# A four-layer graph network in fp32 on one core: order of block products and sums inside the LSTM steps

## The chip, the cores and the metric

The kernel runs on one core of one Trainium2 chip. The metric is the time of one execution on the device in microseconds (us). Five engines work side by side, each through its own list of instructions in order: TensorE (PE in the profile; its weight loads stand as PEld), VectorE (DVE), ScalarE (ACT), GpSimd (POOL) and SyncE (SP), which issues the DMA transfers here. The order of each list is set by the program text: the kernel switches the scheduler off and places every piece by hand.

## The reference, cut to what matters

Four layers, each with layer norm, relu, a graph operation and a residual sum. The change lies in layer 1, two graph convolutions and then, for p = 1 to 4, an LSTM over windows of p tokens whose last state replaces the last token of its window:

```python
h = relu(einsum('ts,bsh->bth', adj, x @ Wg0 + bg0))
h = relu(einsum('ts,bsh->bth', adj, h @ Wg1 + bg1))
for p in range(1, MAX_SKIP + 1):              # MAX_SKIP = 4, H = 256
    nw = Tv // p
    wins = h[:, :nw * p, :].reshape(Bv * nw, p, Hd)
    last = _lstm_last(Wih[p-1], Whh[p-1], bih[p-1], bhh[p-1], wins)
    h = h.at[:, idx, :].set(last.reshape(Bv, nw, Hd))

# one step of the LSTM
g = x_t @ Wih.T + h @ Whh.T + bias
i, f, gg, o = split(g, 4)
c = sigmoid(f) * c + sigmoid(i) * tanh(gg)
h = sigmoid(o) * tanh(c)
```

x has 128 batches of 64 tokens with 256 channels. The kernel cuts them into 16 chunks of 512 columns; two chunks make a superchunk, and the LSTMs of a superchunk run beside the convolutions, residual sums and normalizations of others ("the other stream").

## The kernel before

A gate's product of a 256 x 256 weight matrix with 256 channels is done as seven block products instead of eight, with sums in place of the eighth. A `Unit` is one gate in one step. Gates i and g (numbers 0 and 2) are the A units, f and o (1 and 3) the B units. Each block product has a part with the input x and one with the state h; both go into the same place in PSUM. Products 1, 6, 7 and 4 of a gate accumulate one after another in bank x, product 5 has bank y, products 2 and 3 the halves of bank z. Two banks of each kind are there, so the next gate takes over a bank once its reader is done.

```python
self.of = {1: "x", 6: "x", 7: "x", 4: "x", 5: "y", 2: "z", 3: "z"}

def copy(self, kind):      # ScalarE; kind 1 to block (0, 0), kind 5 to block (1, 1)
    nc.scalar.copy(gate(self.q, kind // 5, halves[kind // 5]), self.psum(kind))

def add(self, dst, a, kind):                                   # VectorE
    nc.vector.tensor_add(gate(self.q, *dst), gate(self.q, *a), self.psum(kind))

def c11(self): self.add((0, halves[0]), (0, halves[0]), 2)     # P1 + P2
def u4(self):  self.add((0, halves[1]), (1, halves[1]), 6)     # P5 + (P1+P6)
def c12(self): self.add((0, halves[1]), (0, halves[1]), 3)     # ... + P3
def c22(self): self.add((1, halves[1]), (1, halves[1]), 7)     # P5 + (P1+P6+P7)
# act(0): ScalarE on c11 and c12; act(1): on c22; act(2): on P1+P6+P7+P4 in PSUM
```

The step, on which all hangs (`each` does one operation for all named units, then the next; `yield` lets the other stream put in a piece):

```python
for s in range(1, p):
    last = s == p - 1
    B = [Unit(q, s) for q in (1, 3)]
    # ... (differences of x for the next step, on GpSimd)
    each(A, pe(5, "h"), do("copy", 5), pe(1), do("copy", 1), pe(3, "h"), pe(6, "x"), pe(6, "h"),
         pe(2, "h"), do("u4"), do("c11"), do("c12"))
    each(B, pe(5), do("copy", 5))
    each(A, do("act", 0), pe(7), do("c22"), do("act", 1))
    each(B[:1], pe(3), pe(2))
    each(A, pe(4), do("act", 2))
    # ... (weights of later steps, when last)
    nc.gpsimd.tensor_mul(gates[:, 0, :, :n], gates[:, 0, :, :n], gates[:, 2, :, :n])
    each(B[1:], pe(3), pe(2))
    each(B, pe(1), do("copy", 1))
    yield
    each(B, pe(6))
    A = [] if last else [Unit(q, s + 1) for q in (0, 2)]
    each(A, pe(5, "x"))

    def cell(c, part):
        nc.vector.tensor_mul(cells[:, c, part], cells[:, c, part], gate(1, c, part))
        nc.vector.tensor_add(cells[:, c, part], cells[:, c, part], gate(0, c, part))
        nc.scalar.activation(gate(2, c, part), cells[:, c, part], AF.Tanh)

    if last:
        each(B[:1], do("u4"), do("c11"), pe(7))
        each(B[1:], do("u4"), pe(7))
        each(B[:1], do("c22"), do("c12"), do("act", 0))
        each(B[1:], do("c22"), do("c11"), do("c12"), do("act", 0))
        cell(0, every)
    else:
        for u in B:
            each([u], do("u4"), do("c11"), do("c12"), do("act", 0))
        cell(0, every)
        each(B, pe(7), do("c22"))
    each(B, do("act", 1))
    each(A[:1], pe(3, "x"), pe(2, "x"))
    new_state(s, 0, every)
    # ... (differences of the state)
    each(A[1:], pe(3, "x"), pe(2, "x"))
    each(B, pe(4))
    B[0].act(2)
    cell(1, halves[1])
    B[1].act(2)
    cell(1, halves[0])
    # ... (the other half's state)
    yield
```

The other stream is placed by the number of the yield. A conversion (`convolutions`) of a chunk goes piece by piece: batch norm and 32 x 32 transposes and a round trip through DRAM; the residual sum; layer norm statistics; its application (twice); a product with the adjacency matrix; its copies; a product with Wg0; a maximum (`bounded`); a product with Wg1; a sum (`biased`); the adjacency again; two relus. `CONV` holds the yields of a superchunk's two chunks, `FIRST` those in the first superchunk, `START` the order of pieces before the first LSTM, `RESIDUAL` those of the residual sum behind the LSTM. With p=1 the yields are 0 to 3, p=2 has 4 to 7, p=3 8 to 13, p=4 14 to 21; even numbers from 6 on are in the middle of a step or in a first product, odd ones at an end.

Of the kernel before, what the change touches and what calls it, by code (L numbers as in the profile page):

```python
# [19 lines left out]
def kernel(  # L20
# [23 lines left out]
    B, T, D = x.shape  # L44
# [544 lines left out]
    with tc.manual_schedule(engines={mybir.EngineType.PE, mybir.EngineType.DVE,  # L589
# [27 lines left out]
        for c in range(2, NCH - 1):  # L617
            a, z = sevens[c], sevens.get(c - 1)
# [146 lines left out]
    with tc.manual_schedule(engines={mybir.EngineType.PE, mybir.EngineType.DVE,  # L765
# [3 lines left out]
        for c in range(2, NCH - 1):  # L769
            a, b, z = sevens[c], sevens.get(c + 1), sevens.get(c - 1)  # L770
# [121 lines left out]
    hTs = {}  # L892
# [146 lines left out]
    def operands_x(p, hv, name, s):  # L1039

        nw, nb, inner, tokens = columns_x(p, hv)
        m = nw * nb // 2
        t = l1.tile([P, 7 * (T // 3) * NB], F32, tag="xd", name=f"xd_{name}_{s}", bufs=2)
        t = [t[:, i * m : (i + 1) * m].rearrange("p (a b) -> p a b", b=inner) for i in range(4)]
        b = {(k, j): tokens(k, s, j) for k in range(KD) for j in range(2)}
        for f in differences(nc.gpsimd, t, b[0, 0], b[0, 1], b[1, 0], b[1, 1]):
            f()
        return {5: t[0], 6: t[1], 7: t[2], 4: t[3], 1: b[0, 0], 2: b[1, 0], 3: b[1, 1]}

    def lstm(p, hv, name, follows, x1, ending):  # L1050
# [3 lines left out]
        n = nb * nw  # L1054
# [32 lines left out]
        halves = [slice(0, m), slice(m, n)]  # L1087
        every = slice(0, n)
# [51 lines left out]
        class Unit:  # L1140
# [31 lines left out]
            def c12(self):  # L1172
                self.add((0, halves[1]), (0, halves[1]), 3)

            def c22(self):
                self.add((1, halves[1]), (1, halves[1]), 7)

# [8 lines left out]
        def each(us, *fs):  # L1186
            for f in fs:
                for u in us:
                    f(u)

        def pe(kind, parts="xh"):
            return lambda u: u.product(kind, parts)

        def do(f, *a):
            return lambda u: getattr(u, f)(*a)

        A = [Unit(q, 1) for q in (0, 2)]
        each(A, pe(5, "x"), pe(3, "x"), pe(2, "x"))
# [3 lines that stand above are left out]
            B = [Unit(q, s) for q in (1, 3)]  # L1202
            if not last:
                ox[s + 1] = operands_x(p, hv, name, s + 1)
            each(A, pe(5, "h"), do("copy", 5), pe(1), do("copy", 1), pe(3, "h"), pe(6, "x"), pe(6, "h"),
                 pe(2, "h"), do("u4"), do("c11"), do("c12"))
            each(B, pe(5), do("copy", 5))
            each(A, do("act", 0), pe(7), do("c22"), do("act", 1))
            each(B[:1], pe(3), pe(2))
            each(A, pe(4), do("act", 2))  # L1210
            if last:
                load_sets(2)
            nc.gpsimd.tensor_mul(gates[:, 0, :, :n], gates[:, 0, :, :n], gates[:, 2, :, :n])  # L1213
            each(B[1:], pe(3), pe(2))
            each(B, pe(1), do("copy", 1))
            yield
            each(B, pe(6))
            A = [] if last else [Unit(q, s + 1) for q in (0, 2)]
            each(A, pe(5, "x"))

            def cell(c, part):
                nc.vector.tensor_mul(cells[:, c, part], cells[:, c, part], gate(1, c, part))
                nc.vector.tensor_add(cells[:, c, part], cells[:, c, part], gate(0, c, part))  # L1223
                nc.scalar.activation(gate(2, c, part), cells[:, c, part], AF.Tanh)  # L1224

            if last:

                each(B[:1], do("u4"), do("c11"), pe(7))
                each(B[1:], do("u4"), pe(7))
                each(B[:1], do("c22"), do("c12"), do("act", 0))  # L1230
                each(B[1:], do("c22"), do("c11"), do("c12"), do("act", 0))
                cell(0, every)
            else:
                for u in B:
                    each([u], do("u4"), do("c11"), do("c12"), do("act", 0))
                cell(0, every)
                each(B, pe(7), do("c22"))
            each(B, do("act", 1))
            each(A[:1], pe(3, "x"), pe(2, "x"))
            new_state(s, 0, every)  # L1240
            if not last:
                dh[0]()
# [6 lines that stand above are left out]
            new_state(s, 1, halves[1])  # L1249
            if not last:  # L1250
                dh[1]()
            new_state(s, 1, halves[0], nc.gpsimd if follows and last else nc.vector)
            if last:
                load_sets(2)
                ending()
            else:
                dh[2]()
            yield
# [145 lines left out]
    def lstms(sc, hT):  # L1404
        hv = hT.rearrange("p k (t b) -> p k t b", t=T)

        names = [f"{sc}_{p}" for p in range(SKIP + 1)]

        def ending(p):

            if p < SKIP:
                operands[p + 1] = operands_x(p + 1, hv, names[p + 1], 1)
            elif sc < NCH // SUP - 1:
                nxt = hTs[sc + 1].rearrange("p k (t b) -> p k t b", t=T)
                operands[1] = block_sums(blocks(sc + 1, nxt), f"{sc + 1}_1")

        yield from single(blocks(sc, hv), names[1], operands.pop(1, None), lambda: ending(1))
        for p in range(2, SKIP + 1):
            yield from lstm(p, hv, names[p], p == SKIP and sc < NCH // SUP - 1, operands.pop(p),
                            lambda: ending(p))  # L1420
# [50 lines left out]

    RESIDUAL = (0, 3, 4), (2, 5, 6)
    CONV = (3, 4, 4, 5, 6, 7, 8, 9, 10, 10), (3, 4, 4, 11, 12, 13, 14, 15, 16, 17, 18, 20)
    BEGUN = (11, 13, 14, 16), (17, 19)
    BEGUN_FIRST = (12, 15, 16, 18), (19, 21)
    FIRST = (1, 3, 3, 4, 4, 5, 6, 7, 8, 9, 10, 11, 12, 12), (3, 6, 7, 8, 10, 13, 14, 15, 16, 17, 18, 19, 20, 20)
    AHEAD = (4, 5, 7, 12, 14, 15), (6, 7)
    LATE = 5, 6, 8, 9  # L1480
    IDLE = {5: 4, 7: 18, 9: 10, 13: 14, 15: 8}
    FINAL = (4, 5, 10, 12, 12, 14), (6, 7, 11, 14, 14, 16)
    START = (0, 1, 0, 0, 0, 1, 0, 1, 1, 0, 0, 1, 1, 0, 1)

    tc.no_sync_barrier()
    with tc.manual_schedule(engines={mybir.EngineType.PE, mybir.EngineType.DVE, mybir.EngineType.Pool,
# [4 lines left out]
        aheads = {c: ahead(c) for c in range(NCH - SUP)}  # L1491
        for n, i in enumerate(START):
            if n == 5:
# [14 lines left out]
    with tc.manual_schedule(engines={mybir.EngineType.PE, mybir.EngineType.DVE, mybir.EngineType.Pool,  # L1508
                                     mybir.EngineType.Activation, mybir.EngineType.SP}):
        last = NCH // SUP - 1  # L1510
        for sc in range(last + 1):
            todo = {}

            def units(places, unit):
                for n in places:
                    todo.setdefault(n, []).append(unit)


            if sc > 1:
                units(LATE[:1], aheads[sc * SUP - 3])  # L1520
            if sc < last:
                for i in range(SUP):
                    units((CONV if sc else FIRST)[i], convs[(sc + 1) * SUP + i])
                new_hT(sc + 1)
            if sc:
                for i in range(SUP):
                    units(RESIDUAL[i], residual((sc - 1) * SUP + i, hTs[sc - 1]))
            else:
                units([0], convs[1])
            if sc > 1:  # L1530
                units(LATE[1:], aheads[sc * SUP - 3])
            if sc:
                for i in range(SUP):
                    units((FINAL if sc == last else AHEAD)[i], aheads[(sc - 1) * SUP + i])
            if sc + 1 < last:
                for i in range(SUP):
                    units((BEGUN if sc else BEGUN_FIRST)[i], convs[(sc + 2) * SUP + i])
            for n, _ in enumerate(lstms(sc, hTs[sc])):
                for u in todo.pop(n, ()):
                    next(u)  # L1540
                if sc == last and n in IDLE:
                    keep_busy(IDLE[n], f"l{n}")
                if sc == last and n == 8:

                    new_hT(sc + 1)
                    for c in range(SUP):
                        load2(c, hTs[sc + 1][:, c, :].rearrange("p (q n) -> p q n", q=Q))
            assert not todo
# [422 lines left out]
    def store(c, t):  # L1971
# [3 lines left out]
        for r in range(2):  # L1975
# [18 lines left out]

    FIRST = """table+0 load2+2 q2+0 copyq2+0 res1+14 res1+15 v2a+0 v2b+0 score2+0 res1+14 res1+15
               exp2+0 q2+1 divide2+0 copyq2+1 load2+3 turn2+0 v2a+1 v2b+1 out2+0 keep+0 res1+14 res1+15
# [15 lines left out]
    with tc.manual_schedule(engines={mybir.EngineType.PE, mybir.EngineType.DVE,  # L2012
                                     mybir.EngineType.Activation, mybir.EngineType.Pool,
                                     mybir.EngineType.SP}):
        run(FIRST, 0)
        close_l1r()
# [61 lines left out]
```

## Time and profile before

| | |
|---|---|
| median of 3 runs | 1889.92 us (1889.86 to 1890.83) |
| span of the profiled execution | 1890.8 us |
| superchunks 1 to 5, from one's p=1 to the next one's | 155.57 us each |
| products of the LSTM steps (L1155) with xd, hd in bank x, 128 columns | 1152 records, 286 and 275 ns |
| weights of the LSTM, DMA | 96 x 960 KB, 6.5 us each |

In the profile L1155 is the product of a unit, L1164 its sum on VectorE, L1161 the copy on ScalarE, L1084 its activation, L1222 and L1223 the cell's multiplication and sum, L1113 the activations of a p's first step, L1126 that step's products. A line of a timeline gives the start, the busy time, engine, line, operation, output and input with shapes, the number of instructions merged, and in brackets the idle time before it and what ended it. TensorE's records overlap: the length of one is not the distance to the next.

### The profile page before, as it was taken

What the parts mean: (1) busy time and instruction counts of PE and PEld (TensorE: products, weight loads), DVE (VectorE), ACT (ScalarE), POOL (GpSimd) and SP (SyncE); (2) the same over time, 40 slices, a digit from 0 to 9 for tenths busy, and PEclk for the clock granted to TensorE, in tenths of its full rate; (3) what the DMA queues carried; (4) which work ended last, traced back from release to release, by engine and by line L of the source; (5) the groups of instructions that cost most, each with busy time, mean ns of one, the idle gap of its engine ahead of it and who ended that gap; (6) DMA issues with size and microseconds to landing.
All of it is one profiled execution on the core that took longest, in us unless ns stands there. A gap on an engine that the chain in (4) does not pass through costs nothing.

```text
span 1890.8 us, 39088 instructions
## 1 busy us (share of the span) xinstructions
PE 1863.0 (99%) x15077; PEld 1479.3 (78%) x15077; DVE 1236.6 (65%) x3150; ACT 1016.6 (54%) x2284; POOL 551.4 (29%) x704
## 2 busy tenths in 40 slices
PE   8999989999999999999999999999999999999998
PEld 6877856886897798699589689878969967777776
DVE  6768845567476666667667666665565567676776
ACT  5766544456456446555655645655565544444453
POOL 5856622122222212212322321222122114332232
PEclk9999999999999999999999999999999999999999
DMA  3224643135333433332433343343144254444433
GB/s 114 73 66 150 234 175 105 49 116 184 106 129 139 151 129 129 110 124 114 151 118 139 141 151 129 129 135 117 52 135 154 71 157 135 143 148 142 139 113 113
DMA packets 111273, 241.45 MB, mean 128 GB/s; under 512 B 11504, under 2 KB 74864, under 8 KB 111088
## 3 DMA queue, kind: packets, MB, share of 16 engines
q1 hardware_dynamic: 110192, 237.09, 37.4%
q8 instruction: 119, 1.95, 0.4%
q0 software_dynamic: 320, 1.05, 0.2%
q10 hardware_dynamic: 576, 0.82, 0.1%
q14 instruction: 66, 0.54, 0.1%
HBM read 170.50 MB, written 68.42 MB: 126 GB/s over the span
## 4 chain that ended last, share of the span: by engine, by line
PE 90%; DVE 5%; ACT 2%; issue 1%; POOL 1%; DMA 1%; SPq 0%; DVEq 0%; ACTq 0%
PE x L1155 23%; PE z L1155 11%; PE g L1126 9%; PE y L1155 6%; PE v L1568 6%; PE x L1329 4%; PE y L1329 3%; PE u L929 3%; PE p_q L1575 3%; PE v L915 3%; PE X L1764 3%; PE X L423 2%; PE X L499 2%; PE Y L1764 1%; PE Y L423 1%
## 5 line engine op out<-in xcount | busy, mean ns | idle before, releaser
L1164 DVE TENSOR_TENSOR gates<-gates,x 128x128 f32<-128x128 f32 (+2 forms) x384 | 118.5, 321 | 326.3 <-PE x L1155 319.1
L1155 PE MATMUL x<-xd,wset 128*128 128x128 f32 (+2 forms) x1152 | 256.8, 311 | 0.7 <-DVE gates L1164 0.2
L1155 PE MATMUL x<-hd,wset 128*128 128x128 f32 (+2 forms) x1152 | 246.7, 303 | 0.0
L1213 POOL TENSOR_TENSOR gates<-gates 128x512 f32<-128x512 f32 (+2 forms) x48 | 75.0, 1562 | 551.8 <-ACT gates L1084 551.8
L1084 ACT ACTIVATE gates<-gates,bias 128x256 f32<-128x256 f32 (+4 forms) x384 | 170.3, 490 | 56.2 <-DVE gates L1164 52.7
L1155 PEld LDWEIGHTS x<-xd,wset 128*128 128x128 f32 x1152 | 180.8, 190 | 19.0 <-DVE gates L1164 6.1
L1155 PEld LDWEIGHTS x<-hd,wset 128*128 128x128 f32 x1152 | 185.1, 191 | 5.0
L1126 PE MATMUL g<-hT,wset 128*128 128x256 f32 (+2 forms) x576 | 183.9, 474 | 1.1 <-DVE hT L1095 1.1
L1126 PEld LDWEIGHTS g<-hT,wset 128*128 128x128 f32 x576 | 108.6, 190 | 69.8 <-issue 38.5
L1161 ACT COPY gates<-y 128x128 f32<-128x128 f32 (+2 forms) x192 | 54.3, 294 | 202.3 <-PE y L1155 201.8
L1155 PE MATMUL z<-hs,wset 128*128 128x128 f32 (+2 forms) x768 | 154.0, 303 | 0.0
L1155 PE MATMUL z<-hT,wset 128*128 128x128 f32 (+2 forms) x768 | 148.4, 306 | 0.0
L1155 PEld LDWEIGHTS z<-hs,wset 128*128 128x128 f32 x768 | 119.8, 191 | 3.3
L1155 PEld LDWEIGHTS z<-hT,wset 128*128 128x128 f32 x768 | 117.9, 192 | 4.4 <-ACT gates L1113 0.5
L1161 ACT COPY gates<-x 128x128 f32<-128x128 f32 (+2 forms) x192 | 56.6, 296 | 93.5 <-PE x L1155 92.8
L1164 DVE TENSOR_TENSOR gates<-gates,z 128x128 f32<-128x128 f32 (+2 forms) x384 | 104.5, 316 | 0.1
L1084 ACT ACTIVATE gates<-x,bias 128x128 f32<-128x128 f32 (+2 forms) x192 | 74.8, 390 | 49.3 <-PE x L1155 46.5
L1113 ACT ACTIVATE gates<-g,bias 128x512 f32<-128x512 f32 (+2 forms) x144 | 74.6, 560 | 30.7 <-PE g L1126 30.2
L1155 PE MATMUL x<-hT,wset 128*128 128x128 f32 (+2 forms) x384 | 85.7, 305 | 0.4 <-ACT gates L1084 0.2
L1155 PE MATMUL x<-hs,wset 128*128 128x128 f32 (+2 forms) x384 | 84.9, 303 | 0.0
L1224 ACT ACTIVATE gates<-cell 128x256 f32<-128x256 f32 (+2 forms) x144 | 55.3, 384 | 51.9 <-DVE cell L1223 50.3
L1155 PE MATMUL y<-xd,wset 128*128 128x128 f32 (+2 forms) x384 | 77.4, 304 | 3.9 <-ACT gates L1113 3.3
(326 smaller groups left out, 4144.6 us busy)
## 6 DMA issues: line engine op xcount, KB each, us to landing
wset<-wfar SPq DMA_DIRECT2D x96, 960.0 KB, 6.5
hT<-far_h SPq DMA_DIRECT2D x124, 128.0 KB, 3.1
far_h<-hm SPq DMA_DIRECT2D x16, 512.0 KB, 2.8
far_n<-xs SPq DMA_DIRECT2D x16, 512.0 KB, 3.5
xs<-far_n SPq DMA_DIRECT2D x64, 128.0 KB, 3.7
far_x<-xs SPq DMA_DIRECT2D x16, 512.0 KB, 3.0
x<-far_x SPq DMA_DIRECT2D x64, 128.0 KB, 3.2
xt<-in_x_dram SPq DMA_DIRECT2D x15, 512.0 KB, 4.1
```

Of the source, the lines that this page charges most:

```text
L423: nc.tensor.matmul(self.banks[tag][:, i * CH // 2 : (i + 1) * CH // 2], w, self.at[kind], start=first and not i, stop=True, skip_group_che ...
L915: nc.tensor.matmul(banks[m], wg0_sb[:, k, m * P : (m + 1) * P], agg[:, k, :], start=(k == 0), stop=(k == KD - 1))
L1084: nc.scalar.activation(gate(q, c, part), src, AF.Tanh if q == 2 else AF.Sigmoid, bias=bs[:, q * KD + c : q * KD + c + 1])
L1113: nc.scalar.activation(columns_of(gate(q, c)), natural(banks[q, c][:, :n].rearrange("p (w b) -> p w b", b=nb)), AF.Tanh if q == 2 else AF. ...
L1126: nc.tensor.matmul(banks[q, c][:, :n].rearrange("p (w b) -> p w b", b=nb), wsets[p, q][:, 2 * k + c, :], hv[:, k, : (nw - 1) * p + 1 : p, ...
L1155: nc.tensor.matmul(folded(self.psum(kind)), wsets[p, self.q][:, BLOCKS[kind][i], :], (ox[self.s] if part == "x" else oh)[kind], start=firs ...
L1161: nc.scalar.copy(gate(self.q, kind // 5, halves[kind // 5]), self.psum(kind))
L1164: nc.vector.tensor_add(gate(self.q, *dst), gate(self.q, *a), self.psum(kind))
L1213: nc.gpsimd.tensor_mul(gates[:, 0, :, :n], gates[:, 0, :, :n], gates[:, 2, :, :n])
L1329: nc.tensor.matmul(folded(ps(g, kind)), wih1[:, g, KINDS1[kind], :], right[kind], start=kind in (2, 5, 1), stop=True, skip_group_check=True)
L1568: nc.tensor.matmul(ps[:, i, :], hT[:, k, j, :], w[:, k, first : first + D], start=(k == 0), stop=(k == KD - 1))
L1764: nc.tensor.matmul(st[c, tag][:, i * CH // 2 : (i + 1) * CH // 2].rearrange("p (a n) -> p a n", n=P), w, st[c, "o7"][kind], start=first an ...
```

## The change

It sets the products and sums of a step in another order; no product is added or removed. For the A units product 2 goes ahead of product 6. For the B units the sums are taken apart: P5 + P3 is formed as soon as P3 is there (`v5`), P1 + P2 (`c11`) as well, and behind product 6 there is one sum alone (`u5`). Product 1 of both goes ahead of products 3 and 2 of the second B unit, so that they stand between products 1 and 6. In the last step product 2 of the second B unit comes behind product 6. The special order of the last step is dropped: sums, activation, product 7, cell and c22 now stand as in the others.

A new yield ("a", counted as a half) behind the A units' products 7 takes VectorE pieces of the other stream that stood at the middle of the step, where they would now be in front of `u5`. In the first superchunk the pieces of chunk 2 begin at the end of `START` instead of at yield 1, and are spread.

```diff
+            def v5(self):
+                self.add((0, halves[1]), (1, halves[1]), 3)
+
+            def u5(self):
+                self.add((0, halves[1]), (0, halves[1]), 6)
@@
-            each(A, pe(5, "h"), do("copy", 5), pe(1), do("copy", 1), pe(3, "h"), pe(6, "x"), pe(6, "h"),
-                 pe(2, "h"), do("u4"), do("c11"), do("c12"))
+            each(A, pe(5, "h"), do("copy", 5), pe(1), do("copy", 1), pe(3, "h"), pe(2, "h"), pe(6), do("u4"),
+                 do("c11"), do("c12"))
             each(B, pe(5), do("copy", 5))
             each(A, do("act", 0), pe(7), do("c22"), do("act", 1))
-            each(B[:1], pe(3), pe(2))
+            yield "a"
+            each(B[:1], pe(3), do("v5"))
             each(A, pe(4), do("act", 2))
@@
-            each(B[1:], pe(3), pe(2))
+            each(B[:1], pe(2))
             each(B, pe(1), do("copy", 1))
+            each(B[:1], do("c11"))
+            each(B[1:], pe(3), do("v5"))
+            if not last:
+                each(B[1:], pe(2), do("c11"))
             yield
             each(B, pe(6))
+            if last:
+                each(B[1:], pe(2))
@@
+            each(B, do("u5"))
             if last:
-                each(B[:1], do("u4"), do("c11"), pe(7))
-                each(B[1:], do("u4"), pe(7))
-                each(B[:1], do("c22"), do("c12"), do("act", 0))
-                each(B[1:], do("c22"), do("c11"), do("c12"), do("act", 0))
-                cell(0, every)
-            else:
-                for u in B:
-                    each([u], do("u4"), do("c11"), do("c12"), do("act", 0))
-                cell(0, every)
-                each(B, pe(7), do("c22"))
+                each(B[1:], do("c11"))
+            each(B, do("act", 0), pe(7))
+            cell(0, every)
+            each(B, do("c22"))
             each(B, do("act", 1))
@@
-    RESIDUAL = (0, 3, 4), (2, 5, 6)
-    CONV = (3, 4, 4, 5, 6, 7, 8, 9, 10, 10), (3, 4, 4, 11, 12, 13, 14, 15, 16, 17, 18, 20)
+    RESIDUAL = (0, 3, 4), (2, 5, 5.5)
+    CONV = (3, 4, 4, 5, 5.5, 7, 8, 9, 10, 10), (3, 4, 4, 11, 11.5, 13, 14, 15, 15.5, 17, 18, 20)
-    FIRST = (1, 3, 3, 4, 4, 5, 6, 7, 8, 9, 10, 11, 12, 12), (3, 6, 7, 8, 10, 13, 14, 15, 16, 17, 18, 19, 20, 20)
+    FIRST = (1, 2, 3, 4, 5, 5.5, 7, 8, 9, 9.5, 11, 12, 12), (3, 5.5, 7, 8, 10, 13, 14, 15, 15.5, 17, 17.5, 19, 20, 20)
-    START = (0, 1, 0, 0, 0, 1, 0, 1, 1, 0, 0, 1, 1, 0, 1)
+    START = (0, 1, 0, 0, 0, 1, 0, 1, 1, 0, 0, 1, 1, 0, 1, 2)
@@
-            for n, _ in enumerate(lstms(sc, hTs[sc])):
+            n = -1
+            for mark in lstms(sc, hTs[sc]):
+                n = n + 0.5 if mark else int(n) + 1
```

## The prediction

> **What bounds the kernel now.** I read the page first: shares of engines, then the chain that ended last.
>
> ```profile
> PE 1863.0 (99%) x15077; PEld 1479.3 (78%) x15077; DVE 1236.6 (65%) x3150; ACT 1016.6 (54%) x2284; POOL 551.4 (29%) x704
> ...
> PE 90%; DVE 5%; ACT 2%; issue 1%; POOL 1%; DMA 1%; SPq 0%; DVEq 0%; ACTq 0%
> ```
>
> TensorE is busy for 99% of the span and carries 90% of the chain. The change removes no product and no sum, so it can only win the time in which TensorE waits. How much is that? The list of waits names few microseconds, so I went to a table of stretches: two of the eight superchunks, and a place in the first one.
>
> ```profile
> 304.00:307.00 3.00, 0.50 (x2) 0.03 (x1) 0.18 (x2) 2.79 (x6) 0.00 (x0) 1.00 0.43 175
> 307.00:311.60 4.60, 4.60 (x16) 2.84 (x16) 2.85 (x5) 3.88 (x7) 0.00 (x0) 0.64 0.76 179
> ...
> 605.68:761.24 155.56, 155.47 (x1091) 126.27 (x1091) 102.03 (x281) 86.75 (x212) 36.36 (x44) 1.00 0.37 131
> 916.81:1072.38 155.57, 155.48 (x1091) 126.28 (x1091) 102.04 (x281) 86.83 (x212) 36.36 (x44) 1.00 0.38 131
> ```
>
> Columns: stretch, length, then PE, PEld, DVE, ACT, POOL with counts, then the granted clock. A superchunk takes 155.56 us, always the same, and PE is busy for 155.47 of it. That is not yet "no waits": a record lasts 0.28 us or longer, while records start 0.11 us apart, so a short wait hides under the record before it. It has to be read from starts. TensorE in the last step of p=4:
>
> ```profile
> 1055.79 0.39 PE L1155 MATMUL x<-hs,wset 128*128 128x128 f32 x2
> 1056.09 0.49 PE L1155 MATMUL x<-xd,wset 128*128 128x128 f32 x2
> ...
> 1056.86 0.39 PE L1155 MATMUL x<-hd,wset 128*128 128x128 f32 x2
> 1057.25 0.49 PE L1155 MATMUL x<-xd,wset 128*128 128x128 f32 x2
> ...
> 1058.02 0.39 PE L1155 MATMUL x<-hd,wset 128*128 128x128 f32 x2
> 1058.34 0.49 PE L1155 MATMUL x<-xd,wset 128*128 128x128 f32 x2
> 1058.67 0.39 PE L1155 MATMUL x<-hd,wset 128*128 128x128 f32 x2
> ```
>
> A product of a block with x or h is two records (passes). Undisturbed pairs start 0.22 us apart. From 1055.79 to 1056.09 it is 0.30 (a wait of 0.07), from 1056.86 to 1057.25 0.39 (0.17), from 1058.02 to 1058.34 0.32 (0.10); and each pair behind a wait takes 0.33, that is 0.10 for starting again. These are P1 to P6 (waits for ScalarE's copy of P1), P6 to P7 (for u4), P7 to P4 (for c22).
>
> I added start-to-start times over the undisturbed 0.112 (128 columns), 0.143 (168), 0.216 (256), over the superchunk at 916.8: 3.66 us lost, of which 0.79 around the convolutions' small products, 0.66 in p=3's steps, 2.07 in p=4's, none in p=2's step; the rest is dust.
>
> VectorE in step 2 of p=4:
>
> ```profile
> 1043.63 0.29 DVE L1164 TENSOR_TENSOR gates<-gates,x 128x128 f32<-128x128 f32 x1 [3.97 <-PE x L1155]
> 1043.84 0.48 DVE L1164 TENSOR_TENSOR gates<-gates,z 128x128 f32<-128x128 f32 x2
> 1044.23 0.28 DVE L1164 TENSOR_TENSOR gates<-gates,x 128x128 f32<-128x128 f32 x1
> 1044.43 0.48 DVE L1164 TENSOR_TENSOR gates<-gates,z 128x128 f32<-128x128 f32 x2
> 1044.89 0.43 DVE L1222 TENSOR_TENSOR cell<-cell,gates 128x256 f32<-128x256 f32 x1
> 1045.42 0.42 DVE L1223 TENSOR_TENSOR cell<-cell,gates 128x256 f32<-128x256 f32 x1
> 1045.76 0.48 DVE L1164 TENSOR_TENSOR gates<-gates,x 128x128 f32<-128x128 f32 x2
> ```
>
> It idles 3.97 us, then has six sums at once (u4, c11, c12 of both B gates), 0.20 us apart, then the cell's two operations, then c22, for which P4 waits. That crowd is what the change thins.
>
> In the first superchunk, the chain:
>
> ```profile
> 304.13 0.06 DVE nmr_b L194
> ...
> 304.72 1.57 ACT cv L196 x3
> 306.29 0.58 ACT gates L1113
> ...
> 307.00 1.18 PE y L1155 x4
> ```
>
> Chunk 2's normalization is late, holds ScalarE, and p=2's first activations release their PSUM banks late: TensorE waits 2.67 us.
>
> **What the Trainium skill says.** "Perfetto Trace Analysis", Identifying the Most-Contended Engine: matmul busy time is no good measure of distance from the limit. The trace agrees: 155.47 busy of 155.56, with 3.66 lost. "TensorE: Matmul & The Clock Gate", What's actually happening: the array falls to half clock after idling for some 3.4 us and needs as long again. Here a wait of 2.67 was enough: the granted clock behind it is 0.64, and eight 256-column passes take 3.46 us in place of 8 x 0.216 = 1.73. "VectorE: DVE Perf Modes", The DRAIN you can't avoid: the next operation starts only when the pipe is empty. The trace shows it less strictly: 128-column sums of 0.28 start 0.20 apart; a dependent pair (mul, add) of 0.43 starts 0.53 apart.
>
> **The change, part by part.** T is the start of the last pass of the first B gate's P6 (gate f, the other is o). Each product is 4 passes.
>
> 1. In steps that are not the last, P3 and P2 of gate o now stand between P1 and P6: 8 passes of 0.112 = 0.89 us more for a copy that was 0.07 late (in the last step P3 alone, 0.45). That wait goes.
>
> 2. VectorE has u5, u5 in place of six sums; P5+P3 and P2 are added before P6. act 0 of f starts after one sum, not three: 2 x 0.20 = 0.40 us sooner, and with it cell and c22. In p=4: P4 is 25 passes after T, 2.79; c22 was done at T+2.79, so 0.06 late; now T+2.41. That wait goes (step 1 of p=3 too, 0.20), and the next step's first waits shrink: at 1047.13 of 0.15 goes, at 1048.32 of 0.30 becomes about 0.2. In p=4's step 2 the wait for u4 behind a conversion (0.32) becomes about 0.1.
> Removed in p=4: three P1-P6 waits (3 x 0.174 = 0.52), two P7-P4 (0.31), 0.22, 0.15 and 0.10; in p=3 two P1-P6 (0.17) and 0.20. Sum 1.67.
>
> 3. The last step of each p (one for p=2, 3, 4) changes against it. Before, c22 stood in front of cell. Now the order is u5, u5, c11 of o (waits for P2, moved behind P6), cell mul, cell add, c22; P4 is only 17 passes after T.
> p=4: P2 of o is complete at 8 x 0.112 + 0.275 = 1.17, c11 starts at 1.21, mul 1.41, add 1.94, c22 2.28 to 2.56, seen by TensorE at 2.62. P4 could start at 1.90: a wait of 0.72 + 0.10. Before: P6-P7 0.27 and P7-P4 0.20, now gone.
> p=3 (pass 0.143, sums 0.32 long and 0.24 apart, mul 0.61 ahead of add): c22 done at 3.09, P4 could start at 2.42: 0.73 + 0.10. Before 0.29.
> p=2 (pass 0.216, sums 0.42 and 0.33 apart, mul to add 0.79): c22 done at 4.30, P4 could at 3.67: 0.68 + 0.10. Before 0.
> New: 0.82 + 0.83 + 0.78 = 2.43; old, gone: 0.47 + 0.29 = 0.76. Cost 1.67.
>
> 4. Convolution sums moved from middle to the "a" place: VectorE reaches them behind A's c22 as before, since B's new sums come later. Zero by itself; without it part 2 would be lost.
>
> 5. A's P2 before P6: u4 has 12 passes before P7 of g in place of 16, 1.3 us for some 0.65. Zero.
>
> So a steady superchunk: -1.67 + 1.67 = 0.0, give or take 0.5.
>
> 6. First superchunk. Chunk 2's conversion (2 x 0.5 and 1.3 us on VectorE, at 286.54) moves to 274.1, where VectorE idles 5.5 us. Its data then lands some 10 us sooner, sums at place 1, statistics at 2; the normalization no longer holds ScalarE. Gone: 2.67 + 0.19 for restarting, the slow passes 3.46 - 1.73 = 1.73, some 0.3 of the wait at 291.38 (0.46). Sum 4.9.
>
> Total: 1889.9 - 4.9 - 8 x 0.0, and 0.5 for the last superchunk, which has bare step starts (one wait of 0.43): 1884.5.
>
> **Rivals.**
> *The last steps hurt more.* If c22 drags the cell chain and the next p's products wait too, 8 x 3 x 0.3 = 7 us come back: 1891 or above. For: VectorE works in order and c11 of o really stands ahead of the cell. Against: behind p=2 and p=3 stand convolution products of 3.4 us.
> *The last steps hurt less, step starts gain more.* If ScalarE and VectorE chains shorten as a whole, the waits of part 3 may be 0.3 each: 24 x 0.5 = 12 us better, 1872 to 1876. For: the six sums were the only crowd. Against: mul and add must come ahead of c22, and they alone take about 0.9 us.
> *First superchunk's wait only moves.* p=3's start there already waits 0.70 behind statistics; if p=2's products now wait for POOL's differences behind the normalization's power (1.18), only 2 to 3 us are won: 1887. Against: by my count those end near 301.5, needed at 304.4.
>
> **Range and chances.** Each of 24 last steps is uncertain by 0.2 in the same direction (5 us), the first superchunk by 1.5: 1878.5 to 1890.5. All that TensorE waits for in the LSTM stage is about 36 us, 1.9%, so 2% faster is out of reach; 2% slower needs 1.6 us in every last step on top.
>
> **What would show it.** A steady superchunk of 155.1 to 156.0; P6 following P1 at the undisturbed pitch; in last steps a wait of 0.7 before P4 of f; the granted clock at 307 being 1.00. A superchunk under 154.5 means that part 3 is wrong; over 156.5, that it spreads; a wait of over 1 us still at p=2's start, that part 6 is wrong.

## The result, and the profile after

| | before | after |
|---|---|---|
| median of 4 runs each, one chip | 1889.89 us (1889.72 to 1890.83) | 1920.97 us (1920.69 to 1921.01) |
| ratio | | 1.0163, 95% interval 1.0145 to 1.0181 |
| one steady superchunk (at 916.8 us before, at 932.8 us after) | 155.57 us | 160.16 us |
| of it lost between starts of products | 3.66 us | 8.25 us |

The change makes the kernel 1.6% slower. The prediction was 1884.5, with 1878.5 to 1890.5 as its range: the result lies 30 us above its end.

The page of the changed kernel, shares of engines and the chain that ended last:

```profile
PE 1861.0 (97%) x15077; PEld 1475.8 (77%) x15077; DVE 1252.2 (65%) x3150; ACT 1022.2 (53%) x2284; POOL 547.6 (29%) x704
...
PE 85%; DVE 9%; ACT 2%; issue 2%; POOL 1%; DMA 0%; DVEq 0%; SPq 0%; ACTq 0%
```

TensorE does the same 15077 instructions in 1861.0 us (1863.0 before), but its share of the chain falls from 90% to 85%, and VectorE's rises from 5% to 9%. The span is 28 us longer (1918.9 for 1890.8: the LSTM stage is 32.2 us longer, and the later layers are 3.9 us shorter, see the last section), and what was added are waits of TensorE for VectorE. The stretches (columns as in the prediction: PE, PEld, DVE, ACT, POOL, clock) say where:

```profile
303.00:306.00 3.00, 3.00 (x13) 2.27 (x12) 2.52 (x5) 2.07 (x4) 0.00 (x0) 1.00 0.23 71
...
932.77:1092.94 160.17, 155.89 (x1092) 126.02 (x1091) 103.84 (x281) 87.59 (x212) 35.98 (x44) 1.00 0.37 127
```

The second row is a superchunk; the other steady ones are as long, 4.6 us longer than before. The first row is the place in the first superchunk where the kernel before waited 2.67 us and then ran at a clock of 0.64: here TensorE is busy throughout, at full clock. So the part that was counted on works, and something repeats in every superchunk that was not counted at all. The list of waits names it: TensorE's waits for VectorE's sums, with their total in us, their number and the longest. (The list counts only the time in which no record of TensorE runs, so a short wait is missing from it.)

```profile
PE x L1155 <- DVE gates L1164: 19.3, 28, 1.6
...
PE z L1155 <- DVE gates L1164: 17.5, 39, 0.7
```

In the kernel before the first of these rows was 0.2 us, once, and the second was not there. A product in bank x behind a sum is product 4, which waits for c22, or product 7; those of product 4 in the last steps were expected. A product in bank z behind a sum is new. This is gate o in step 1 of p=4 in the kernel before, where the last two passes of product 3 and the first two of product 2 follow each other at 0.22:

```profile
1026.73 0.39 PE L1155 MATMUL z<-hs,wset 128*128 128x128 f32 x2
1026.95 0.39 PE L1155 MATMUL z<-hT,wset 128*128 128x128 f32 x2
```

The same place in the changed kernel, TensorE and VectorE:

```profile
1047.10 0.39 PE L1155 MATMUL z<-hT,wset 128*128 128x128 f32 x2
...
1047.32 0.39 PE L1155 MATMUL z<-hs,wset 128*128 128x128 f32 x2
1047.74 0.29 DVE L1164 TENSOR_TENSOR gates<-gates,z 128x128 f32<-128x128 f32 x1 [0.31 <-PE z L1155]
...
1048.09 0.49 PE L1155 MATMUL z<-hT,wset 128*128 128x128 f32 x2 [0.38 <-DVE gates L1164]
```

The passes at 1047.10 and 1047.32 are product 3. The sum at 1047.74 is v5, P5 + P3. Product 2, at 1048.09, should follow product 3 at 1047.54, and starts 0.54 later, when v5 is done; another 0.10 goes by its restart (its second pair starts at 1048.41, 0.32 behind, in place of 0.22). Product 2 needs nothing of v5. But products 2 and 3 are the two halves of one bank z, and v5 reads one half: the kernel holds the write of product 2 into the other half until that read has ended.

From starts of products, over the superchunk at 932.8, six such waits are new: p=2 0.82 + 0.10; p=3 0.58 + 0.10 and 0.31 + 0.10; p=4 0.60, 0.54 and 0.54, each + 0.10. Together 4.0 us, of the 4.6 that a superchunk grew. For gate o it is the bare way there and back (product 3 ends, v5 runs, product 2 starts: 0.54 at 128 columns). For gate f eight passes of the A units stand between, and still it waits in three of the six steps, because there v5 of f stands behind what was put to place a (in this cut the other stream's sum, L935); these three are 2.0 of the 4.0 us:

```profile
1044.12 1.28 DVE L935 TENSOR_TENSOR cv<-u,c 128x512 f32<-128x512 f32 x2
...
1045.32 0.28 DVE L1164 TENSOR_TENSOR gates<-gates,z 128x128 f32<-128x128 f32 x1
...
1045.65 0.49 PE L1155 MATMUL z<-hT,wset 128*128 128x128 f32 x2 [0.43 <-DVE gates L1164]
```

The last step of p=4, the same place as in the prediction:

```profile
1077.97 0.39 PE L1155 MATMUL x<-hd,wset 128*128 128x128 f32 x2
1078.90 0.49 PE L1155 MATMUL x<-xd,wset 128*128 128x128 f32 x2 [0.55 <-DVE gates L1164]
```

and VectorE in it, behind the two u5 (L1235 and L1236 are the cell's multiplication and sum in this kernel):

```profile
1077.50 0.29 DVE L1164 TENSOR_TENSOR gates<-gates,z 128x128 f32<-128x128 f32 x1
1077.70 0.42 DVE L1235 TENSOR_TENSOR cell<-cell,gates 128x256 f32<-128x256 f32 x1
1078.22 0.43 DVE L1236 TENSOR_TENSOR cell<-cell,gates 128x256 f32<-128x256 f32 x1
1078.57 0.48 DVE L1164 TENSOR_TENSOR gates<-gates,x 128x128 f32<-128x128 f32 x2
```

c11, mul, add, c22, and product 4 waits from 1078.19 to 1078.90: 0.71 + 0.10, as worked out (0.72 + 0.10).

### The profile page after: what moved, and what is told of

Same layout as the page of the kernel before. It is cut to its first block, busy times and chain, and to the rows that moved or that the text cites. A ratio compares the mean times of both kernels' runs of the same rounds, so it can differ in the third digit from the quotient of the medians.

```text
span 1918.9 us, 39091 instructions
## 1 busy us (share of the span) xinstructions
PE 1861.0 (97%) x15077; PEld 1475.8 (77%) x15077; DVE 1252.2 (65%) x3150; ACT 1022.2 (53%) x2284; POOL 547.6 (29%) x704
## 4 chain that ended last, share of the span: by engine, by line
PE 85%; DVE 9%; ACT 2%; issue 2%; POOL 1%; DMA 0%; DVEq 0%; SPq 0%; ACTq 0%
PE x L1155 19%; PE z L1155 11%; PE g L1126 9%; PE v L1577 5%; PE y L1155 5%; PE x L1336 4%; PE y L1336 3%; PE u L929 3%; PE p_q L1584 3%; PE v L915 3%; PE X L1773 3%; PE X L423 2%; PE X L499 2%; DVE gates L1164 2%; PE Y L1773 1%
## 5 line engine op out<-in xcount | busy, mean ns | idle before, releaser
L1155 PE MATMUL x<-hd,wset 128*128 128x128 f32 (+2 forms) x1152 | 254.6, 303 | 0.0
L1155 PEld LDWEIGHTS x<-xd,wset 128*128 128x128 f32 x1152 | 186.6, 191 | 34.5 <-DVE gates L1164 30.0
L1164 DVE TENSOR_TENSOR gates<-gates,z 128x128 f32<-128x128 f32 (+2 forms) x384 | 110.9, 319 | 149.2 <-ACT gates L1161 92.9
L1155 PE MATMUL z<-hs,wset 128*128 128x128 f32 (+2 forms) x768 | 146.5, 303 | 0.2 <-DVE hs L1093 0.2
L1155 PE MATMUL y<-hd,wset 128*128 128x128 f32 (+2 forms) x384 | 79.3, 309 | 0.0
```

The lines of the kernel that those rows point to most:

```text
L1155: nc.tensor.matmul(folded(self.psum(kind)), wsets[p, self.q][:, BLOCKS[kind][i], :], (ox[self.s] if part == "x" else oh)[kind], start=firs ...
```

## The experiments

The theory after this reading: v5 between products 3 and 2 costs 4.0 us per superchunk, the last steps some 2.2, and the rest of the change is a gain. Times are given with their ratio to the kernel before on the same chip, where it took 1891.4 to 1891.9; "superchunk" is the distance between two p=1 starts in the trace.

### r1_p2_with_p3: product 2 directly behind product 3

```diff
-            each(B[:1], pe(3), do("v5"))
+            each(B[:1], pe(3), pe(2), do("v5"))
@@
-            each(B[:1], pe(2))
             each(B, pe(1), do("copy", 1))
@@
-            each(B[1:], pe(3), do("v5"))
-            if not last:
-                each(B[1:], pe(2), do("c11"))
+            if last:
+                each(B[1:], pe(3), do("v5"))
+            else:
+                each(B[1:], pe(3), pe(2), do("v5"), do("c11"))
```

> The changed kernel with product 2 of the B units directly behind product 3 again, both ahead of the sums that read bank z (in the last step product 2 of gate o stays behind product 6). Theory (bank): product 2 waits because the sum v5 still reads the other half of the same PSUM bank; seven waits per superchunk, 0.926 + 0.689 + 0.413 + 0.698 + 0.646 + 0.644 = 4.02 us in six places (0.413 is p=3's second step), vanish: superchunk 160.16 to about 156.1, total 1921 - 8 x 4.0 = 1889. Rival (buffer): bank z is late because its earlier user, an A gate, still holds it; then the wait moves from product 2 to product 3 and the time stays at 1915 to 1922. Rival (crowded VectorE): only the waits of gate f behind the pieces at the place a go, 2.0 of the 4.0: about 1905.

Measured: 1904.04 us (1903.56 to 1904.79), ratio 1.0066 (1.0051 to 1.0081), superchunk 157.67. The time is the one that was named for the rival of a crowded VectorE (1905), but its mechanism is not what the trace shows: that rival leaves the waits of gate o, and the waits before product 2 are gone for both gates. Of 4.0 us only 2.5 came back because new waits appeared, which I had not foreseen. Step 1 of p=4, TensorE:

```profile
1033.20 0.39 PE L1155 MATMUL x<-hd,wset 128*128 128x128 f32 x2
1033.60 0.49 PE L1155 MATMUL x<-hT,wset 128*128 128x128 f32 x2
```

Product 1 of gate f (1033.60) now follows product 4 of the A units at once and takes over their bank x, which ScalarE's act 2 still reads: 0.17 + 0.10, three times in p=4, less in p=3. With a wait before product 4 that grows from 0.27 to 0.40 in step 1 of p=4, this is the missing 1.5 us. In the changed kernel product 2 of f, moved behind the A units' product 4, stood just there as a filler. So that move had a use. It suggests that the order of TensorE is good and only the sum's place is wrong, which r5 tests.

### r3_last_c22_first: c22 ahead of the cell in the last step

```diff
-            each(B, do("act", 0), pe(7))
-            cell(0, every)
-            each(B, do("c22"))
+            if last:
+                each(B, pe(7), do("c22"), do("act", 0))
+                cell(0, every)
+            else:
+                each(B, do("act", 0), pe(7))
+                cell(0, every)
+                each(B, do("c22"))
```

> The changed kernel with c22 ahead of the cell in the last step of each p, as it was before; product 2 stays apart from product 3. Theory: the waits before product 4 (0.785 in p=2, 0.897 in p=3, 0.812 in p=4, 2.49 us per superchunk) shrink to about 0.3 in all: 1921 - 8 x 2.2 = 1903. Rival (the cell's chain is what counts, and a later cell delays the next p): no gain, 1918 to 1923.

Measured: 1904.47 us (1904.07 to 1905.1), ratio 1.0069 (1.0052 to 1.0086), superchunk 157.98: 2.19 us less than in the changed kernel. The last step's part has the size that was predicted for it.

### r4_both_mended: r1 and r3 together

> Both repairs: product 2 directly behind product 3, c22 ahead of the cell in the last step. If both theories hold the gains add up: 1921 - 32 - 18 = 1871, a superchunk near 153.9, faster than the kernel before by 1.0%. If the two waits stand in for each other (TensorE waits for the same late VectorE in either place), about 1889.

Measured: 1887.24 us (1885.88 to 1887.67), ratio 0.9977 (0.9968 to 0.9986), superchunk 155.48. 2.50 and 2.19 add up (160.16 - 155.48 = 4.68 against 4.69): neither wait stands in for the other. The superchunk misses the expected 153.9 by the new waits of r1.

### r2_first_superchunk: only chunk 2's pieces, in the kernel before

```diff
-    FIRST = (1, 3, 3, 4, 4, 5, 6, 7, 8, 9, 10, 11, 12, 12), ...
+    FIRST = (1, 2, 3, 4, 5, 6, 7, 8, 9, 10, 11, 12, 12), ...
-    START = (0, 1, 0, 0, 0, 1, 0, 1, 1, 0, 0, 1, 1, 0, 1)
+    START = (0, 1, 0, 0, 0, 1, 0, 1, 1, 0, 0, 1, 1, 0, 1, 2)
```

> The kernel before with the new start alone: chunk 2's conversion begins at the end of the start, its next pieces at yields 1, 2, 3, 4; nothing else of the change. Theory: 1889.9 - 4.9 = 1885.0 (the wait of 2.67 us at p=2's start, its restart and the slow clock behind it go, superchunks stay at 155.57). Rival (the wait only moves to GpSimd's differences or to p=3's start): 1887 or above.

Measured: 1887.02 us (1885.78 to 1887.83), ratio 0.9976 (0.9967 to 0.9985), which is -4.7 us. (The 1887 of the rival is met only because the kernel before takes 1891.7 us on this chip and not 1889.9.) The same point of superchunk 1's p=1 comes at 445.75 (before at 450.12), and a steady superchunk takes 155.56. The wait of 2.67 at p=2's start, the slow clock behind it and the wait at 291.38 are gone; p=3's start still waits 0.70, as before.

### r5_sums_behind_p2: only two sums moved, TensorE's order as in the changed kernel

```diff
-            each(B[:1], pe(3), do("v5"))
+            each(B[:1], pe(3))
@@
-            each(B[:1], pe(2))
+            each(B[:1], pe(2), do("v5"))
@@
-            each(B[1:], pe(3), do("v5"))
-            if not last:
-                each(B[1:], pe(2), do("c11"))
+            if last:
+                each(B[1:], pe(3), do("v5"))
+            else:
+                each(B[1:], pe(3), pe(2), do("v5"), do("c11"))
```

> TensorE's order is that of the changed kernel, unchanged; only VectorE's v5 (and c11 behind it) of the B units is placed behind product 2 of its gate. Theory (bank: product 2 is held until v5 has read the other half of its bank): all six waits before product 2 go and, unlike with product 2 moved forward, product 1 has product 2 of f ahead of it as in the changed kernel, so nothing new comes: a superchunk of 156.1 us, total 1921 - 32 = 1889. Rival (TensorE's order itself is at fault): 160, 1921.

Measured: 1890.87 us (1890.55 to 1892.26), ratio 1.0001 (0.9992 to 1.0009), superchunk 156.26. The waits of bank z for sums have gone from the list; those of bank x are still there, 34 of them with 21.0 us.

TensorE's list of instructions is that of the changed kernel. Only sums on VectorE stand later, and 30 us are back. That settles where the time went.

### r10_p2_in_another_bank: is it the bank, or the sum's place?

r5 takes the sum away from product 2; it doesn't show that the bank is what joins them. In this run the order of every engine stays that of the changed kernel, v5 between products 3 and 2, and only the place of product 2 of the B gates changes, from bank z to the free half of bank y:

```diff
-                self.banks, self.of = {}, {1: "x", 6: "x", 7: "x", 4: "x", 5: "y", 2: "z", 3: "z"}
+                self.banks, self.of = {}, {1: "x", 6: "x", 7: "x", 4: "x", 5: "y", 2: "yz"[q % 2 == 0], 3: "z"}
@@
-    return self.banks[...][:, m:n] if kind == 3 else ...
+    return self.banks[...][:, m:n] if kind == 3 or (kind == 2 and self.of[2] == "y") else ...
```

> The changed kernel with one edit: product 2 of the B gates goes into the unused half of bank y (in which product 5 stands, long since copied) instead of the half of bank z beside product 3. The order on every engine stays that of the changed kernel; v5 still stands ahead of product 2. Theory (product 2 is held because v5 reads the same bank): the six waits before product 2 go, 4.0 us per superchunk, as when v5 was moved behind it: superchunk 156.2, total about 1890. Rival, that the order itself (v5 early in VectorE's list) costs the time wherever product 2 goes: superchunk stays at 160.1, total 1921.

Measured: 1893.40 us (1892.29 to 1894.66), ratio 1.0011 (1.0004 to 1.0018), superchunk 156.13. Step 1 of p=4, gate o, as above:

```profile
1028.84 0.39 PE L1155 MATMUL z<-hs,wset 128*128 128x128 f32 x2
...
1029.06 0.39 PE L1155 MATMUL y<-hT,wset 128*128 128x128 f32 x2
...
1029.26 0.29 DVE L1164 TENSOR_TENSOR gates<-gates,z 128x128 f32<-128x128 f32 x1 [0.31 <-PE z L1155]
1029.29 0.39 PE L1155 MATMUL y<-hs,wset 128*128 128x128 f32 x2
```

Product 2 (1029.06, now in y) follows product 3 at 0.22, and v5 (1029.26) reads bank z beside it. So the two are joined by the shared bank z, and not by the order. (Each bank is one tile of the program here; the runs don't tell whether the program sets the wait for the bank or for the tile.) The Trainium skill has the rule, in "PSUM — Partial Sum Buffer", PSUM bank collisions raise a hardware error: two engines must not touch one bank on the same partitions at once, disjoint columns included, so "Semaphore-guard PSUM by bank × quadrant". The kernel's waits follow it, and here this one costs 4.0 us per superchunk. What the chip would do without the wait was not tried. (The total is 2.5 us above r5's although the superchunk is shorter: in the traces that lies behind the LSTMs, see the last section.)

### r6_and_c22_first: r5 and r3 together

> As the run before, and c22 ahead of the cell in the last step. Theory: the gains add, as the two waits lie in different parts of a step: 156.1 - 2.2 = 153.9 us per superchunk, total 1871 to 1873, which beats the kernel before by 1%. If they stand in for each other: 1887 or above.

Measured: 1874.75 us (1874.35 to 1875.15), ratio 0.9911 (0.9896 to 0.9926), superchunk 154.09. The two mends add up again (3.90 + 2.17), and the result is 0.9% faster than the kernel before (part of that lies outside of the LSTMs, see the last section). Lost between starts are 2.17 us per superchunk, of which 0.50 before product 4 of p=4's step 1 and 0.32 before product 7 of the A units in its step 2.

### r8_without_place_a: place a undone

r6 (the "second run" of the text below) with the residual sum and the conversion's pieces back at 6, 12 and 16 in place of 5.5, 11.5 and 15.5; the first superchunk keeps its place a.

> As the second run of this call (sums behind product 2, c22 first), but the VectorE pieces of the other stream are put back from the place a to the middle of the step. Theory of the prediction's part 4 (the place a costs nothing and keeps u5 in time): 1.4 to 2.4 us of pieces stand ahead of u5 in three steps, P7 waits 0.4 to 0.8 in each: a superchunk longer by 1.5 to 2, total 1883 to 1888. Rival (the place a is itself the cause of the loss): faster than the second run, below 1871.

Measured: 1890.49 us (1889.86 to 1891.27), ratio 0.9994 (0.9986 to 1.0003), superchunk 156.76: 2.67 more than r6. New waits stand before product 7 in p=2 (0.89), p=3 (0.38) and step 1 of p=4 (0.86), behind VectorE's pieces ahead of u5, and the wait before product 4 there grows from 0.40 to 0.63. So place a is needed for the new order, more than I had put it at.

### r7_and_pieces_moved, r11_application_to_place_a, r9_two_pieces_to_place_a: the last two waits

In r6 ScalarE's application at yield 16 (1.2 us) stands ahead of act 0, and VectorE's conversion at 17 (2.4 us) ahead of u4. The three runs, each r6 with one table changed, move them:

```diff
r6    BEGUN = (11, 13, 14, 16), (17, 19)
r7    BEGUN = (11, 13, 14, 17), (17.5, 19)
r11   BEGUN = (11, 13, 14, 17.5), (17, 19)
r9    BEGUN = (11, 13, 14, 17.5), (17.5, 19.5)
```

> As the run before, and two pieces of the other stream moved in p=4: the normalization's application of the even chunk from yield 16 to 17, the conversion of the odd chunk from 17 to 17.5. Theory: in p=4's first step ScalarE's two applications (1.2 us) stand ahead of act 0, and P4 waits 0.27 to 0.40 + 0.10; in the second step VectorE's conversion (2.3 us) holds u4, and P7 waits 0.22 + 0.10. Both go: 0.7 us per superchunk, 153.2, total some 1867. Rival (these waits come from GpSimd or the state's chain): same as the run before.

Measured: 1886.99 us (1885.03 to 1888.03), ratio 0.9975 (0.9965 to 0.9985), superchunks of 155.9 to 158.6. Both waits went, and two worse ones came. ScalarE at the start of p=4's step 2:

```profile
1035.63 1.09 ACT L196 ACTIVATE cv<-xs,nmr_b,rstd_b 128x256 f32<-128x256 f32 x2 [1.49 <-DVE nmr_b L194]
...
1036.93 0.44 ACT L1161 COPY gates<-x 128x128 f32<-128x128 f32 x2
```

At a step's end the application waits for VectorE, and the copies of product 1, which free bank x for product 6, stand behind it: 1.23 us. And VectorE in step 3:

```profile
1051.69 1.29 DVE L284 TENSOR_TENSOR xs<-xs,cv 128x512 f32<-128x512 f32 x2 [1.90 <-DMA xs<-in_x_dram]
```

The conversion left later, so its data came back later, and the residual sum at 19 held u4 by waiting for it: 1.39 us here, and 1.27 to 2.31 us in the five superchunks that have it.

> r6_and_c22_first with only the application of chunk 0 moved, from the middle of p=4's step 1 to place a of its step 2. Theory: only the wait of 0.40 + 0.10 before product 4 of step 1 goes: superchunk 153.6, total 1871 to 1872; the difference to r9 is the conversion's part (0.32 per superchunk). Rival as for r9: the application holds act 2 of the A units, 1875 or more.

Measured: 1875.98 us (1875.6 to 1876.87), ratio 0.9922 (0.9907 to 0.9937), superchunk 154.34. The wait of 0.40 is gone, but product 1 of gate f waits 0.77 in step 2: the application stands ahead of act 2 of the A units, which frees bank x. That was the rival. (In r1 it was product 1, too, that waited in this way, and not product 4 as the next text says.)

> r6_and_c22_first with three pieces of the coming conversions moved to place a: the application of chunk 0 from the middle of p=4's step 1 to place a of its step 2, the conversion of chunk 1 from the end of step 1 to the same place a, its residual sum from the end of step 2 to place a of step 3. In r7_and_pieces_moved the application at a step's end held ScalarE ahead of the next step's copies of product 1 (1.23 us), and the residual sum reached VectorE before its data did (1.39 us). At a place a neither should be in front of anything. Theory: the waits of 0.40 + 0.10 (product 4 of step 1) and 0.22 + 0.10 (u4 of step 2) of r6 go and none comes: superchunk 153.3, total 1869 to 1870. Rival, that the application now holds act 2 of the A units and through it bank x, as product 4 waited in r1_p2_with_p3: superchunk 154 or more, 1875 or more.

Measured: 1873.47 us (1873.29 to 1873.63), ratio 0.9908 (0.9893 to 0.9923), superchunk 153.83. With the conversion out of the way nmr comes sooner and the application holds act 2 for 0.46 only; of the 0.82 hoped for 0.26 is left. It is the fastest of all, though by the intervals not to be told from r6.

### r12_first_superchunk_place_a: the same in the first superchunk

In r9 the first superchunk takes 157.6 us, counted between the same product of its own p=1 and the next one's, and a steady one 153.8. The first one's conversion at 12 and statistics at 16 are still at the middle of a step, ahead of u5:

```diff
-    BEGUN_FIRST = (12, 15, 16, 18), (19, 21)
+    BEGUN_FIRST = (11.5, 15, 15.5, 18), (19, 21)
```

> r9_two_pieces_to_place_a with two pieces of the first superchunk moved from the middle of a step to its place a: the conversion of chunk 4 (p=3's last step) and its statistics (p=4's step 1). In the changed kernel and in r6 and r9 these two stayed at the middle, where they stand in front of u5: product 7 waits 1.34 + 0.10 and 1.71 + 0.10 us there, in the first superchunk alone. Theory: that is why the first superchunk takes 157.6 us in r9, 3.8 more than a steady one, where the kernel before with the first superchunk's pieces moved (r2) had only 0.9 more. The first wait goes; of the second some 0.6 may stay, because another piece of 1.3 us is at the same place. First superchunk 155.0 to 155.5, total 1871. Rival, that the pieces are too much for VectorE wherever they stand: 157 or more, total 1873 as r9.

Measured: 1877.11 us (1876.65 to 1877.7), ratio 0.9923 (0.9907 to 0.994). The wait of 1.34 went and that of 1.71 became 0.82, as expected. But the first superchunk is longer, 161.0 us. TensorE in p=4's first products, and SyncE's queue before it:

```profile
383.73 2.81 PE L1126 MATMUL g<-hT,wset 128*128 128x256 f32 x8 [3.76 <-DMA wset<-wfar]
```

```profile
371.27 0.32 SPq L247 DMA_DIRECT2D far_y<-ym  x1
374.01 1.74 SPq L254 DMA_DIRECT2D cv<-far_y  x4
...
376.33 2.22 SPq L887 DMA_DIRECT2D wset<-wfar  x4
```

In r9 the first two of these weight loads (L887) are asked for at 369.92, ahead of the conversion's write (375.39). In r12 the conversion's write and its read back, which waits for the write, stand in front of them on SyncE's queue: the weights are asked for 6.4 us later, and TensorE waits 3.9 us for them; after that eight passes start 0.43 apart in place of 0.22. The expectation looked at VectorE alone.

## Why the prediction was wrong

**The step that failed is in part 2: "P5+P3 and P2 are added before P6".** It counted these sums on VectorE, where there was time for them, and let TensorE run on through products 3 and 2. In its place the runs showed that TensorE stands still there: v5 reads bank z between the two, and product 2, which writes the other half of it, waits for v5, six times and 4.0 us per superchunk. r5 (the sums moved, -3.9 us per superchunk) and r10 (the bank changed, -4.0) both give back what was lost. From the first LSTM product to the last the trace takes 1242.1 us before, 1274.3 after, and 1244.4 in r5: 29.9 of the 32.2 us come back in r5. The rivals missed it too: they speak of sums that come too late for their own products, none of a product that waits for a sum that it has nothing to do with. One half of it was there to be read, as the description of the kernel before says that products 2 and 3 have the halves of one bank z, and that the next gate takes over a bank once its reader is done. The step that was missing is that a reader holds the other half of its bank as well.

**Part 1: right.** No product 6 waits for the copy of product 1 any more in p=3 and p=4.

**Part 2, the rest: partly right.** Waits before product 4 in step 2 of p=4 and step 1 of p=3 are gone, and of step 3's first waits 0.31 (0.25 predicted). Two stayed. In step 1 of p=4, P7 to P4 is 0.27 + 0.10, where 0.06 + 0.10 was to go: ScalarE's application at yield 16 stands ahead of act 0, so act 0 doesn't come 0.40 sooner there. The u4 wait of step 2 (0.32) is unchanged; it is the conversion alone that sets it. So about 0.5 of the 1.67 did not come.

**Part 3: right in mechanism and size.** Predicted waits before product 4 of the last steps 0.82, 0.83 and 0.78 for p=4, 3, 2; measured 0.81, 0.90 and 0.78, together 2.49 for 2.43. r3 takes 2.19 of it away. It was accepted in the prediction as balanced by part 2, and r6 shows that it need not be paid.

**Part 4: half right.** "Without it part 2 would be lost" is true (r8: 2.67 us). "Zero by itself", because VectorE's new sums come later, is not: the pieces at place a stand ahead of v5 of gate f, and product 2 of f waits for that in three steps, 2.0 of the 4.0 us. They cost this only together with the shared bank; no run has the early v5 without place a, so the share is read from the trace alone.

**Part 5: right;** no wait of product 7 of the A units is new.

**Part 6: right for what it names:** -4.9 predicted, -4.4 in the trace of r2 and -4.7 in its time, clock 1.00. But in the changed kernel the first superchunk is not shorter: that point of superchunk 1's p=1 comes at 452.28, later than before (450.12). Besides the waits of the steady ones it has others, above all 1.34 and 1.58 before product 7, because its conversion and statistics, at 12 and 16 as before, now stand in front of u5. Part 4 would have said so, had it been applied to all tables of pieces.

**The sum.** For a steady superchunk parts 1 and 2 came to -1.2 (predicted -1.67) and part 3 to 2.49 - 0.76 = +1.7 (+1.67). With the missing +4.0 this is +4.5, of +4.6 measured. A steady superchunk was to be 155.1 to 156.0, and "over 156.5" was read as "it spreads": that reading was wrong too, part 3 stayed where it was.

## What to carry to other kernels

When a sum is moved between two products, look at what else lies in the bank that it reads. Here a product into the other half of that bank waited until the sum was done, for 0.54 us and 0.10 for the restart where nothing stood between, and for 0.31 to 0.82 us in all. Either put both products in front of their readers (r5), or put them in different banks (r10). And count a move of work for every engine and queue that it feeds: products also served as fillers (r1), an earlier conversion also put its transfers ahead of the weights (r12), and a later one let the next sum wait for data (r7).

## What the runs showed of the hardware

A sum that reads one bank and a product that writes another run beside each other at full pitch (r10: 0.22 from pair to pair with v5 in between); so the 0.54 us of the changed kernel don't come from VectorE and TensorE being at work in PSUM at the same time.

The time of the later layers, which no run here changes, has several values in the traces: from the LSTMs' last product to the last product of the kernel it is 369.8 us in the kernel before, 369.4 in r2 and 369.7 in r10, 366.0 in the changed kernel, 365.9 in r5 to r9, r11 and r12, and 366.2, 367.4 and 367.1 in r3, r1 and r4. The chain of the kernel before shows one of the places:

```profile
1623.86 0.93 PE s L1843 x62
1624.79 1.14 issue
```

The last two of these 64 small products come behind that. In the changed kernel the chain has the same 64 in one piece of 0.93 us, at 1655.84. TensorE stands still for 1.1 us with nothing in the trace that it waits for; in the three kernels of 369 us and more two products stand over 1 us apart at three places, in r1 and r4 at one, and in the others nowhere over 0.8 us. What it is stays open.

It bears on the totals. In the traces r10 spends 3.8 us more than r5 behind the LSTMs, which is why its total is above r5's while its superchunk is shorter. Of the 17.6 us between the spans of r6 and the kernel before, the LSTMs give 14.1 and the later layers 3.9, so r6's 0.9% is not all its own; and r5, level with the kernel before in total, is 2.3 us longer in the LSTMs. Whether the kernel before varies by 3 us from one execution to the next for the same reason is not shown, as there is one trace of it.
